# The slot numbers' broadcast moved, c split into two tiles, and the last two tiles added and stored by banks

## The chip, the cores and the metric

The kernel runs on one core of a Trainium2 chip. Its time is the device time of one execution in microseconds (us), the median of several runs. TensorE (PE) multiplies, VectorE (DVE), ScalarE (ACT) and GpSimd (POOL) do the rest, and SyncE (SP), ACT and POOL issue the DMAs.

## The reference

The input x has 8 batches of 512 rows with 2048 columns. Two layers and a residual follow, all in fp32:

```python
# layer 1: one linear map and a low-rank adapter that each batch picks by its slot number
base_out = einsum('bti,oi->bto', x, W) + b
A = lora_As[adapter_mapping]; Bm = lora_Bs[adapter_mapping]      # rank 16, 32 slots
y = base_out + einsum('btr,bro->bto', einsum('bti,bir->btr', x, A), Bm) * 2.0
# layer 2: 8 experts of rank 16; each row takes the one with the largest logit
logits = einsum('bsd,ed->bse', y, route_w)
topk_v, topk_idx = top_k(logits, 1)
route_weight = one_hot(topk_idx[..., 0], 8) * topk_v
h = einsum('bsd,erd->bser', y, A_ffn)
out = x + einsum('bser,eor->bso', route_weight[..., None] * h, Bw)
```

The kernel never builds y. What layer 2 wants of y are 136 numbers a row (128 of h and 8 logits), and these are linear in x. So W is folded into the 136 projections once (c, 2048 x 136), and each row tile is multiplied with c. The output is x plus a product of 128 numbers a row with Bw.

## The kernel before, in words

**Start.** POOL issues the broadcast of the eight slot numbers to all partitions (it_i, line 92), then fills an identity and three index tables. SP loads W in 16 chunks of 128 rows (1 MB each, load_w, line 103) and, between them, the projections (pj). ACT and DVE each reorder one half of every chunk (chunk_w, line 286), and PE folds it (fold_w, line 297) into the six PSUM tiles pc of the pool ps_c, one bank each. Beside this, from chunk 4 on, the slot numbers become row indices (line 165), by which POOL gathers the adapters. At chunk 11 DVE places the adapters A of batches 0 and 1 in c (line 379). At the last chunk the six pc tiles are copied into c (the tile cm, line 307), in turn by ACT and DVE: five with three column blocks each, the sixth with one. Then the pools of the fold close and ps_h (two banks) and ps_o (two tiles of two banks) open on the banks of ps_c; ps_s keeps its two.

**Main loop.** There are 32 row tiles, two half steps each; n counts the half steps, h is the half. For a tile t: the 16 products with c (heads, line 409), DVE's turn of the low-rank part (turn_low) and its addition on PE (add_low, line 433), DVE's choice of the expert (route, lines 446 to 454, which ends with wh), PE's transpose of wh (turn_heads, line 464, pw), ACT's copy of it (keep_heads, line 469, whT), the product with Bw in two halves of 1024 columns (delta, line 492), DVE's addition to x (add_delta, line 505) and the store (line 516). POOL and ACT shuffle quadrants of x (line 254) and DVE transposes them (line 239) for later tiles. Every two tiles SP loads x (line 122).

**Order.** The whole kernel stands under `manual_schedule`: each engine issues its instructions in the order in which the Python code emits them. What one engine waits for of another is derived from the tiles. Within one half step the order is:

```python
        if h == 0 and 0 < t <= NT:
            route(t - 1)
        tp, hp = piece(n - 1)
        if tp >= 0:
            add_delta(tp, hp)
        turn_x(t + 1, h)
        if h == 1 and 0 < t <= NT:
            keep_heads(t - 1)
```

Then come the shuffles, turn_low and delta. In the steps n = 63 and 64 a call stands between the first and the second product of delta: add_low(31), and turn_heads(31).

**End.** Tile 30 is added in halves of 1024 columns and stored by SP in halves. Tile 31 (the last) has its two halves cut into pieces in single banks: 512 and 512 columns in two banks of ps_h, then 512, 256 and 256 in ps_o, ps_o and ps_s. Each piece is added and stored by itself; the stores alternate between SP and ACT.

Of the kernel before, what the change touches and what calls it, by code (L numbers as in the profile page):

```python
# [9 lines left out]
F32 = mybir.dt.float32  # L10
# [8 lines left out]
def kernel(  # L19
# [29 lines left out]
    nc = tc.nc  # L49
    P = 128  # L50
    Q = 32
    NQ = P // Q
    B, T, D = x.shape
# [4 lines left out]
    R = ER // E  # L58
    NJ = D // P
# [3 lines left out]
    NT = B * TPB  # L63
# [4 lines left out]
    HN = D // 512 // 2  # L68
    NA = NP + R
    assert B * R == P and ER == P and DO == D and B == 2 * NQ  # L70

    const = ctx.enter_context(tc.tile_pool(name="const", bufs=1))
# [7 lines left out]
    ps_s = ctx.enter_context(tc.tile_pool(name="ps_s", bufs=2, space=bass.MemoryType.PSUM))  # L80
# [8 lines left out]


    it_i = const.tile([P, B], I32, name="it_i")
    nc.gpsimd.dma_start(out=it_i, in_=itok.to_broadcast([P, B]))
    pj = wpool.tile([P, NO, NP], F32, name="pj")
    proj_v = proj.rearrange("(c p) e -> p c e", p=P)

# [118 lines left out]
    def fill_constants():  # L214

        nc.vector.memset(one, 0.0)
        nc.vector.memset(one[:, :, R : R + 1], 1.0)

        nc.vector.tensor_reduce(
            own4, mask.rearrange("p (g h) -> p g h", h=2), AX.X, ALU.add  # L220
        )
        for k in range(2):
            h = const.tile([P, NQ, Q], F32, name=f"hls_{k}")
            nc.vector.memset(h, 0.0)
            nc.vector.tensor_copy(h[:, :, R : R + 1], own4.unsqueeze(2))
            hls.append(h)

    cm = const.tile([P, NJ, NA + R], F32, name="cm")  # L230
    ad_aT = const.tile([P, NJ, P], F32, name="ad_aT")
    ad_bT = tpool.tile([P, NJ, P], F32, tag="t", name="ad_bT")
    g4 = const.tile([P, B, NP], F32, name="g4")
# [58 lines left out]
    def fold_w(oc):  # L292
        for q, (pc, (j0, n)) in enumerate(zip(pcs, groups)):
            for k in range(n):

                h, j = divmod(j0 + k, HJ)
                nc.tensor.matmul(  # L297
                    pc[:, k, :],
                    wv_tiles[oc, h][:, j, :],
                    pj[:, oc, :],  # L300
                    start=(oc == 0 and k == 0),
                    stop=(oc == NO - 1),
                    skip_group_check=True,
                )
            if oc == NO - 1:
                copy = nc.scalar.copy if q % 2 == 0 else nc.vector.tensor_copy
                copy(cm[:, j0 : j0 + n, R:NA], pc[:, :n, :])  # L307


    bp = wpool.tile([P, NP], F32, name="bp")  # L310
# [42 lines left out]
    for oc in range(NO):  # L353
        if oc + 1 < NO:
            chunk_w(oc + 1)
        fold_w(oc)
        if oc == 2:
            fill_constants()
        if oc == 4:
            load_adapters_b()  # L360
        if oc == 7:
            load_adapters_a()
        if 8 <= oc < 12:
            turn_adapters(oc - 8)
        if oc in (9, 10):
            fold_bias(range(8 * (oc - 9), 8 * (oc - 8)))
        if oc == 8:
            load_x(0)
            shuffle(0, moves[6:], nc.gpsimd.tensor_copy)
        if oc == 11:  # L370
            nc.sync.dma_start(out=fb, in_=ffn_b)
            load_x(1)
            load_x(2)
            project_bias()
        if oc in (10, 11):
            turn(ad_aT, ad_ar, oc - 10)
        if oc == 11:
            for b in range(2):
                nc.vector.tensor_copy(cm[:, :, ds(b * NA, R)], ad_aT[:, :, ts(b, R)])
        if oc == 12:  # L380
            project_adapters()
        if oc in (12, 13, 14):
            shuffle(0, moves[2 * (oc - 12) : 2 * (oc - 11)], nc.scalar.copy)
        if oc == 14:
            for h in range(2):
                turn_x(0, h)
    wctx.close()
    ps_h = ctx.enter_context(tc.tile_pool(name="ps_h", bufs=2, space=bass.MemoryType.PSUM))
# [10 lines left out]
    po_tiles = {}  # L399
# [4 lines left out]
    def heads(t, j0, j1):  # L404
        s = batch_of(t) % 2
        if j0 == 0:
            ph_tiles[t] = ps_h.tile([P, 512], F32, tag="h", name=f"ph_{t}")[:, :NA]
        for j in range(j0, j1):
            nc.tensor.matmul(  # L409
                ph_tiles[t],  # L410
                xT_tiles[t][:, j, :],
                cm[:, j, ds(s * R, NA)],
                start=(j == 0),
                stop=(j == NJ - 1),
            )
# [15 lines left out]
    def add_low(t):  # L431
        b = batch_of(t)
        nc.tensor.matmul(  # L433
            ph_tiles[t][:, ds((1 - b % 2) * R, NP)],
            hT_tiles.pop(t),
            g4[:, b, :],
            start=False,
            stop=True,
            skip_group_check=True,
        )  # L440
# [21 lines left out]
    def turn_heads(t):  # L462
        pw = ps_s.tile([P, P], F32, tag="s", name=f"pw_{t}")
        nc.tensor.transpose(pw, wh_tiles.pop(t), ident)  # L464
        pw_tiles[t] = pw

    def keep_heads(t):
        whT_tiles[t] = small.tile([P, P], F32, tag="whT", name=f"whT_{t}")
        nc.scalar.copy(whT_tiles[t], pw_tiles.pop(t))  # L469

    def delta(t, h, within=None):

        c0 = h * D // 2
        if t < NT - 1:
            po = ps_o.tile([P, HN, 512], F32, tag="o", name=f"po_{t}_{h}")
            cuts = [(512, po[:, k, :]) for k in range(HN)]
            adds = [(ds(c0, D // 2), po.rearrange("p n d -> p (n d)"))]
        else:

            def bank(pool, tag, n):  # L480
                shape = [P, HN, 512] if tag == "o" else [P, 512]
                b = pool.tile(shape, F32, tag=tag, name=f"pe_{tag}")
                return n, (b[:, 0, :] if tag == "o" else b)[:, :n]

            if h == 0:
                cuts = [bank(ps_h, "h", 512), bank(ps_h, "h", 512)]
            else:
                cuts = [bank(ps_o, "o", 512), bank(ps_o, "o", 256), bank(ps_s, "s", 256)]
            adds = []
        c = c0  # L490
        for n, part in cuts:
            nc.tensor.matmul(part, whT_tiles[t], fb[:, ds(c, n)], start=True, stop=True)  # L492
            if t == NT - 1:
                adds.append((ds(c, n), part))
            c += n
            if within:
                within()
                within = None
        po_tiles[t, h] = adds

    def add_delta(t, h):
        u, k = divmod(t, TPU)
        for m, (cols, part) in enumerate(po_tiles.pop((t, h))):
            xs = x_tiles[u][:, k, cols]
            nc.vector.tensor_tensor(xs, xs, part, ALU.add)  # L505
            if t == NT - 1:
                store(t, cols, nc.scalar if m % 2 else nc.sync)
        if t == NT - 2:
            store(t, ts(h, D // 2))
        elif t < NT - 2 and h == 1:  # L510
            store(t, ds(0, D))

    def store(t, cols, eng=nc.sync):
        u, k = divmod(t, TPU)
        b, r = divmod(t, TPB)
        eng.dma_start(out=out[b, ts(r, P), cols], in_=x_tiles[u][:, k, cols])

    def piece(n):

        return divmod(n - 3, 2) if 0 <= n - 3 < 2 * NT else (-1, -1)  # L520
# [15 lines left out]
    for n in range(2 * NT + 4):  # L536
        t, h = divmod(n, 2)
        if t < NT:

            heads(t, h * HJ, h * HJ + HJ // 2)  # L540
            if n == 2:
                add_low(0)
            if n == 3:
                turn_heads(0)
            heads(t, h * HJ + HJ // 2, (h + 1) * HJ)
# [8 lines that stand above are left out]
        u, ms = shuffle_slot(n)  # L554
        shuffle(u, ms, nc.gpsimd.tensor_copy if n == 2 else nc.scalar.copy)
        if h == 1 and t < NT:
            turn_low(t)
        last = n in (2 * NT - 1, 2 * NT)
        if last:

            delta(*piece(n), (lambda: add_low(t)) if h else (lambda: turn_heads(t - 1)))
        elif piece(n)[0] >= 0:
            delta(*piece(n))
        if h == 1 and 0 < t < NT and not last:
            add_low(t)
        if h == 1 and t < NT:
            b, k = divmod(t, TPB)
            if k == 0 and 0 < b < B - 1:
                nc.gpsimd.tensor_copy(
                    cm[:, :, ds((b + 1) % 2 * NA, R)], ad_aT[:, :, ts(b + 1, R)]  # L570
                )
        if h == 0 and 1 < t <= NT and not last:
            turn_heads(t - 1)
        tq, hq = piece(n - 5)
        u, k = divmod(tq, TPU)
        if tq >= 0 and hq == 1 and k == TPU - 1 and u + XB < NU:
            load_x(u + XB)
# [48 lines left out]
```

## Time and profile before

| what | us |
|---|---|
| median of 3 runs | 334.65 (334.64 to 334.68) |
| the profiled execution's own time | 334.58 |
| its span | 332.8 |
| PE busy | 323.9 |
| DVE busy | 233.7 |
| ACT busy | 171.0 |
| POOL busy | 136.3 |
| PE idle between W's first and second chunk | 1.14 |
| PE idle between the fold and the first head product | 0.48 |
| from the last add's start to the end of the span | 5.8 |

A line of the timeline gives the start, the duration, the engine, the line of the code, the operation, what it writes and reads with shapes, how many instructions are merged in it, and in brackets how long the engine was idle before it and what ended that. PEld are the weight loads of PE. A name with q, such as ACTq, is the engine's sequencer, here issuing a DMA. All times in the text are from the start of the span.

### The profile page before, as it was taken

Reading aid. Unit: us, or ns where it says so; the run is one execution under the profiler, and the core shown is the slowest. Engines: PE = TensorE matmul, PEld = TensorE weight load, DVE = VectorE, ACT = ScalarE, POOL = GpSimd, SP = SyncE. Lnnn points to the kernel's source line nnn. Section 1 sums busy time; section 2 is a strip of 40 time slices with the busy share of each in tenths; the row PEclk is TensorE's granted clock in tenths of the full one; section 3 lists DMA queues with packets and bytes.
Section 4 is the critical chain, followed back from the end, with each engine's and each line's share of the span. In section 5 each row is a group of like instructions: output and inputs, shape, how many; then the busy total and the mean of one; then the engine's idle time right before and its main releaser. Section 6 shows DMA issues by size and latency. Waiting matters only on the chain.

```text
span 332.8 us, 5119 instructions
## 1 busy us (share of the span) xinstructions
PE 323.9 (97%) x1968; PEld 260.4 (78%) x1968; DVE 233.7 (70%) x425; ACT 171.0 (51%) x193; POOL 136.3 (41%) x143
## 2 busy tenths in 40 slices
PE   8899999999999999999999999999999999999992
PEld 8899999999777777777777777777777777777751
DVE  1133386476877877887878888888878777877753
ACT  3223236646857548565656575757566576630000
POOL 2001503989781609263535536262809081600000
PEclk9999999999999999999999999999999999999999
DMA  7999999958633394857676675849493949333336
GB/s 218 399 405 418 420 407 424 418 221 306 272 161 142 119 391 147 373 173 331 214 292 251 255 291 214 325 183 366 171 376 161 378 174 392 130 126 128 127 145 234
DMA packets 15800, 88.83 MB, mean 267 GB/s; under 512 B 1680, under 2 KB 4640, under 8 KB 5536
## 3 DMA queue, kind: packets, MB, share of 16 engines
q1 hardware_dynamic: 14544, 85.80, 65.7%
q0 software_dynamic: 528, 2.11, 2.0%
q10 hardware_dynamic: 704, 0.60, 0.6%
q8 instruction: 15, 0.25, 0.3%
q14 instruction: 9, 0.07, 0.1%
HBM read 54.88 MB, written 33.62 MB: 266 GB/s over the span
## 4 chain that ended last, share of the span: by engine, by line
PE 94%; DMA 3%; DVE 0%; ACT 0%; SPq 0%; issue 0%; DVEq 0%
PE ph L409 40%; PE po L492 32%; PE pc L297 17%; DMA w<-in_w_dram 3%; PE ph L433 2%; PE pg L342 1%; PE pw L464 1%; PE pbT L324 1%; PE pe_h L492 1%; ACT wv L286 0%; DVE x L505 0%; PE pe_o L492 0%; SPq L103 0%; DVEq L622 0%; DVE cm L307 0%
## 5 line engine op out<-in xcount | busy, mean ns | idle before, releaser
L254 POOL COPY xq<-x 32x1024 f32<-32x1024 f32 x121 | 126.2, 1043 | 118.2 <-DMA x<-in_x_dram 83.9
L254 ACT COPY xq<-x 32x1024 f32<-32x1024 f32 x135 | 140.9, 1043 | 17.9 <-DMA x<-in_x_dram 11.1
L409 PE MATMUL ph<-cm,xT 128*128 128x152 f32 x1024 | 142.6, 293 | 0.5 <-DVE cm L307 0.5
L409 PEld LDWEIGHTS ph<-cm,xT 128*128 128x128 f32 x1024 | 135.1, 190 | 9.3 <-issue 8.7
L492 PE MATMUL po<-fb,whT 128*128 128x512 f32 x248 | 116.7, 592 | 0.0
L505 DVE TENSOR_TENSOR x<-x,po 128x1024 f32<-128x1024 f32 x62 | 75.0, 1210 | 5.6 <-PE po L492 5.5
L239 DVE STREAM_TRANSPOSE xT<-xq 128x1024 f32<-128x1024 f32 x64 | 78.8, 1235 | 0.1
L492 PEld LDWEIGHTS po<-fb,whT 128*128 128x128 f32 x248 | 43.2, 190 | 29.2 <-issue 28.9
L297 PE MATMUL pc<-pj,wv 128*128 128x136 f32 x512 | 60.7, 279 | 1.5 <-ACT wv L286 1.1
L297 PEld LDWEIGHTS pc<-pj,wv 128*128 128x128 f32 x512 | 59.8, 190 | 1.9 <-ACT wv L286 1.3
L469 ACT COPY whT<-pw 128x128 f32<-128x128 f32 x32 | 8.5, 266 | 88.7 <-PE pw L464 88.7
L286 DVE COPY wv<-w 128x1024 f32<-128x1024 f32 (+1 forms) x17 | 13.5, 799 | 29.9 <-PE pc L297 16.1
L446 DVE TENSOR_REDUCE top<-ph 128x1 f32<-128x8 f32 x32 | 5.3, 167 | 37.5 <-PE ph L433 37.5
L286 ACT COPY wv<-w 128x1024 f32<-128x1024 f32 (+1 forms) x17 | 16.8, 996 | 27.9 <-DMA w<-in_w_dram 20.6
L433 PEld LDWEIGHTS ph<-g,hT 128*128 128x128 f32 x64 | 12.0, 190 | 15.0 <-issue 12.2
L452 DVE TENSOR_SCALAR rw<-rank,win,top 128x8 f32<-128x8 f32 x32 | 15.5, 484 | 1.2
L433 PE MATMUL ph<-g,hT 128*128 128x136 f32 x64 | 12.7, 280 | 0.0
L428 DVE STREAM_TRANSPOSE hT<-hls 128x128 f32<-128x128 f32 x32 | 10.0, 311 | 1.1
L173 POOL DMA_INDIRECT raw<-in_cond_b_dram,brow_i x1 | 1.0, 1032 | 23.6 <-DVE brow_i L172 23.6
L464 PEld LDWEIGHTS pw<-ident,wh 128*128 128x128 f32 x32 | 4.5, 140 | 7.7 <-issue 5.0
L454 DVE TENSOR_TENSOR wh<-ph,rw 128x128 f32<-128x128 f32 x32 | 9.3, 292 | 1.1
L464 PE MATMUL pw<-ident,wh 128*128 128x128 f32 x32 | 8.7, 273 | 0.0
(70 smaller groups left out, 81.1 us busy)
## 6 DMA issues: line engine op xcount, KB each, us to landing
x<-in_x_dram SPq DMA_DIRECT2D x32, 1024.0 KB, 8.9
out_dram<-x SPq DMA_DIRECT2D x30, 1024.0 KB, 4.8
w<-in_w_dram SPq DMA_DIRECT2D x16, 1024.0 KB, 11.8
fb<-in_ffn_b_dram SPq DMA_DIRECT2D x1, 1024.0 KB
out_dram<-x SPq DMA_DIRECT2D x2, 512.0 KB, 2.6
pj<-in_proj_dram SPq DMA_DIRECT2D x2, 272.0 KB, 11.4
out_dram<-x SPq DMA_DIRECT2D x2, 256.0 KB, 3.1
g<-g_dram SPq DMA_DIRECT2D x4, 68.0 KB, 2.5
```

The source lines that it names most:

```text
L239: nc.vector.transpose(dst[:, ts(h, HJ), :].rearrange("p j (g t) -> p g j t", t=Q), src.rearrange("p g (j a) -> p g j a", a=Q)[:, :, ts(h, ...
L254: copy(xq_tiles[u][ts(i, Q), :, g, :], x_tiles[u][ts(g, Q), :, ts(i, DQ)])
L286: copy(dst[:, ts(k, n)], wr[:, ds(h * HJ + k * n, n)])
L297: nc.tensor.matmul(pc[:, k, :], wv_tiles[oc, h][:, j, :], pj[:, oc, :], start=(oc == 0 and k == 0), stop=(oc == NO - 1), skip_group_check= ...
L409: nc.tensor.matmul(ph_tiles[t], xT_tiles[t][:, j, :], cm[:, j, ds(s * R, NA)], start=(j == 0), stop=(j == NJ - 1),)
L428: nc.vector.transpose(hT, h.rearrange("p g s -> p (g s)"))
L433: nc.tensor.matmul(ph_tiles[t][:, ds((1 - b % 2) * R, NP)], hT_tiles.pop(t), g4[:, b, :], start=False, stop=True, skip_group_check=True,)
L452: nc.vector.tensor_scalar(rw, rank, win, top, ALU.is_equal, ALU.mult)
L454: nc.vector.tensor_tensor(wh.rearrange("p (e r) -> p e r", r=R), ph[:, :ER].rearrange("p (e r) -> p e r", r=R), rw.unsqueeze(2).to_broadca ...
L464: nc.tensor.transpose(pw, wh_tiles.pop(t), ident)
L492: nc.tensor.matmul(part, whT_tiles[t], fb[:, ds(c, n)], start=True, stop=True)
L505: nc.vector.tensor_tensor(xs, xs, part, ALU.add)
```

## The change

It has three parts.

- The issue of the broadcast it_i moves from the head of the program to the point behind fold_w(2), after fill_constants. It stays on POOL.
- c becomes two tiles, one with the first 12 column blocks and one with the last 4. Each head product reads the tile that its block is in. Placing an adapter in c takes two copies instead of one: on DVE for batches 0 and 1, on POOL for the six others.
- The last two tiles, 30 and 31, are both added and stored by pieces in single banks, and a table says which pools these come from. The stores alternate between SP and ACT by the piece's place in its call of add_delta. The first piece of (30, 0) is added and stored right after its delta, in step 63; the second follows in step 64 after route(31), where its place in the call is 0 again.

```diff
-    nc.gpsimd.dma_start(out=it_i, in_=itok.to_broadcast([P, B]))
...
+    JC = NJ * 3 // 4
+    cms = [const.tile([P, n, NA + R], F32, name=f"cm_{n}") for n in (JC, NJ - JC)]
+
+    def cm(j):
+        return cms[j // JC][:, j % JC, :]
+
+    def place_a(b, copy):
+        for k, part in enumerate(cms):
+            n = part.shape[1]
+            copy(part[:, :, ds(b % 2 * NA, R)], ad_aT[:, ds(k * JC, n), ts(b, R)])
...
-                copy(cm[:, j0 : j0 + n, R:NA], pc[:, :n, :])
+                copy(cms[j0 // JC][:, ds(j0 % JC, n), R:NA], pc[:, :n, :])
...
         if oc == 2:
             fill_constants()
+            nc.gpsimd.dma_start(out=it_i, in_=itok.to_broadcast([P, B]))
...
-                nc.vector.tensor_copy(cm[:, :, ds(b * NA, R)], ad_aT[:, :, ts(b, R)])
+                place_a(b, nc.vector.tensor_copy)
...
-                cm[:, j, ds(s * R, NA)],
+                cm(j)[:, ds(s * R, NA)],
...
+    def bank(tag, n):
+
+        pool, shape = {
+            "h": (ps_h, [P, 512]), "s": (ps_s, [P, 512]), "o": (ps_o, [P, HN, 512])
+        }[tag]
+        b = pool.tile(shape, F32, tag=tag, name=f"pe_{tag}")
+        return n, (b[:, 0, :] if tag == "o" else b)[:, :n]
+
+
+    ends = {
+        (NT - 2, 0): (("o", 512), ("o", 512)),
+        (NT - 2, 1): (("h", 512), ("s", 512)),
+        (NT - 1, 0): (("h", 512), ("o", 512)),
+        (NT - 1, 1): (("o", 512), ("h", 256), ("s", 256)),
+    }
+
     def delta(t, h, within=None):
 
         c0 = h * D // 2
-        if t < NT - 1:
+        if (t, h) in ends:
+            cuts = ends[t, h]
+        else:
             po = ps_o.tile([P, HN, 512], F32, tag="o", name=f"po_{t}_{h}")
             cuts = [(512, po[:, k, :]) for k in range(HN)]
...
+            po_tiles[t, h] = [(ds(c0, D // 2), po.rearrange("p n d -> p (n d)"))]
         c = c0
-        for n, part in cuts:
+        for cut in cuts:
+            if (t, h) in ends:
+                cut = bank(*cut)
+                po_tiles.setdefault((t, h), []).append((ds(c, cut[0]), cut[1]))
+            n, part = cut
             nc.tensor.matmul(part, whT_tiles[t], fb[:, ds(c, n)], start=True, stop=True)
...
+    def add_delta(t, h, n=None):
+
         u, k = divmod(t, TPU)
-        for m, (cols, part) in enumerate(po_tiles.pop((t, h))):
+        pieces = po_tiles[t, h]
+        po_tiles[t, h] = pieces[n:] if n else []
+        for m, (cols, part) in enumerate(pieces[:n]):
             xs = x_tiles[u][:, k, cols]
             nc.vector.tensor_tensor(xs, xs, part, ALU.add)
-            if t == NT - 1:
+            if (t, h) in ends:
                 store(t, cols, nc.scalar if m % 2 else nc.sync)
-        if t == NT - 2:
-            store(t, ts(h, D // 2))
-        elif t < NT - 2 and h == 1:
-            store(t, ds(0, D))
+            elif h == 1:
+                store(t, ds(0, D))
...
             delta(*piece(n), (lambda: add_low(t)) if h else (lambda: turn_heads(t - 1)))
+            if h == 1:
+                add_delta(*piece(n), 1)
...
-                nc.gpsimd.tensor_copy(
-                    cm[:, :, ds((b + 1) % 2 * NA, R)], ad_aT[:, :, ts(b + 1, R)]
-                )
+                place_a(b + 1, nc.gpsimd.tensor_copy)
```

More of the change, by code (lines that the diff above doesn't have):

```diff
@@ L226, in fill_constants @@
             hls.append(h)
-    cm = const.tile([P, NJ, NA + R], F32, name="cm")
+    JC = NJ * 3 // 4
[6 more added lines that the diff above has]
+            copy(part[:, :, ds(b % 2 * NA, R)], ad_aT[:, ds(k * JC, n), ts(b, R)])
     ad_aT = const.tile([P, NJ, P], F32, name="ad_aT")
@@ L469, in keep_heads @@
         nc.scalar.copy(whT_tiles[t], pw_tiles.pop(t))
+    def bank(tag, n):
[10 more added lines that the diff above has]
+    }
     def delta(t, h, within=None):
         c0 = h * D // 2
-        if t < NT - 1:
+        if (t, h) in ends:
+            cuts = ends[t, h]
+        else:
             po = ps_o.tile([P, HN, 512], F32, tag="o", name=f"po_{t}_{h}")
             cuts = [(512, po[:, k, :]) for k in range(HN)]
[L477 to L489, printed above, removed]
-        c = c0
-        for n, part in cuts:
+            po_tiles[t, h] = [(ds(c0, D // 2), po.rearrange("p n d -> p (n d)"))]
+        c = c0
+        for cut in cuts:
[3 more added lines that the diff above has]
+            n, part = cut
             nc.tensor.matmul(part, whT_tiles[t], fb[:, ds(c, n)], start=True, stop=True)
-            if t == NT - 1:
-                adds.append((ds(c, n), part))
             c += n
@@ L498, in delta @@
                 within = None
-        po_tiles[t, h] = adds
-    def add_delta(t, h):
+    def add_delta(t, h, n=None):
         u, k = divmod(t, TPU)
-        for m, (cols, part) in enumerate(po_tiles.pop((t, h))):
+        pieces = po_tiles[t, h]
+        po_tiles[t, h] = pieces[n:] if n else []
+        for m, (cols, part) in enumerate(pieces[:n]):
             xs = x_tiles[u][:, k, cols]
             nc.vector.tensor_tensor(xs, xs, part, ALU.add)
-            if t == NT - 1:
+            if (t, h) in ends:
                 store(t, cols, nc.scalar if m % 2 else nc.sync)
-        if t == NT - 2:
-            store(t, ts(h, D // 2))
-        elif t < NT - 2 and h == 1:
-            store(t, ds(0, D))
+            elif h == 1:
+                store(t, ds(0, D))
     def store(t, cols, eng=nc.sync):
```

## The prediction

> **What bounds the kernel now.** The page first: its busy times, then the chain that ended last.
>
> ```profile
> PE 323.9 (97%) x1968; PEld 260.4 (78%) x1968; DVE 233.7 (70%) x425; ACT 171.0 (51%) x193; POOL 136.3 (41%) x143
> ...
> PE 94%; DMA 3%; DVE 0%; ACT 0%; SPq 0%; issue 0%; DVEq 0%
> ```
>
> TensorE is the chain from 11.42 us to 326.05 us, so only three places are open: before 11.42, a gap at 73, and what follows 326.05. The change has one edit in each. I then read the timeline of each place. The start:
>
> ```profile
> 1.28 0.72 POOL L92 DMA_DIRECT2D it_i<-in_itok_dram  x1 [0.83 <-POOLq L611]
> ...
> 10.32 1.05 ACT L286 COPY wv<-w 128x1024 f32<-128x1024 f32 x1 [3.35 <-DMA w<-in_w_dram]
> ...
> 11.42 14.75 PE L297 MATMUL pc<-pj,wv 128*128 128x136 f32 x125 [1.14 <-ACT wv L286]
> ...
> 21.42 1.05 ACT L286 COPY wv<-w 128x1024 f32<-128x1024 f32 x1 [3.63 <-DMA w<-in_w_dram]
> ```
>
> PE stands 1.14 us for W's second chunk, which comes at 10.32. The table of stretches (PE, PEld, DVE, ACT, POOL, clock, DMA share, GB/s) and the queues of the same 1.5 us say why:
>
> ```profile
> 4.00:5.50 1.50, 1.50 (x14) 1.50 (x14) 0.00 (x0) 0.00 (x0) 0.00 (x0) 1.00 1.02 419
> 5.50:7.00 1.50, 1.17 (x11) 0.98 (x10) 0.76 (x2) 1.14 (x2) 0.00 (x0) 1.00 1.07 54
> ```
>
> ```profile
> q0 software_dynamic: 16, 0.00, 90.7%
> ```
>
> The DMA engines are fully busy but move 54 GB/s instead of 419: the broadcast's 16 packets (one an engine, 256 bytes) hold them for 0.907 x 1.5 = 1.36 us. They begin at 5.57, which is 3.57 us after POOL finished the issue at 2.00.
>
> The gap at 73:
>
> ```profile
> 72.79 0.50 ACT L307 COPY cm<-pc 128x408 f32<-128x408 f32 x1 [0.89 <-PE pc L297]
> 73.02 0.30 DVE L307 COPY cm<-pc 128x136 f32<-128x136 f32 x1 [0.34 <-PE pc L297]
> ...
> 73.47 5.41 PE L409 MATMUL ph<-cm,xT 128*128 128x152 f32 x40 [0.48 <-DVE cm L307]
> ```
>
> The end:
>
> ```profile
> 320.81 0.17 DVE L446 TENSOR_REDUCE top<-ph 128x1 f32<-128x8 f32 x1 [0.59 <-PE ph L433]
> ...
> 322.14 0.14 PEld L464 LDWEIGHTS pw<-ident,wh 128*128 128x128 f32 x1 [0.48 <-DVE wh L454]
> ...
> 322.69 0.27 ACT L469 COPY whT<-pw 128x128 f32<-128x128 f32 x1 [4.79 <-PE pw L464]
> ...
> 323.30 1.88 PE L492 MATMUL pe_h<-fb,whT 128*128 128x512 f32 x4
> 323.50 1.22 DVE L505 TENSOR_TENSOR x<-x,po 128x1024 f32<-128x1024 f32 x1 [0.28 <-PE po L492]
> ...
> 325.95 1.53 ACTq L516 DMA_DIRECT2D out_dram<-x  x2
> ```
>
> whT of tile 31 is ready at 322.96, 0.34 us before PE can use it. After 324 the stores fill the DMA engines without a break (352, 381 and 310 GB/s in the three 2-us stretches from 324). The last is issued at 327.45, its packets run from 329.33 to 330.38, it lands at 330.99, the span ends at 332.77. An unhindered store has its first packet 0.83 us after its issue (323.25 to 324.08), so the last one queued about 1.0 us.
>
> **What the Trainium skill says.** "PSUM — Partial Sum Buffer", Engine vs sequencer instructions: the queues of ScalarE, VectorE and GpSimd are strictly first in, first out. "DMA: Bandwidth & Descriptors", Anatomy of one DMA: a DMA's semaphore wait takes place on the sequencer that issues it. Together: an instruction behind a store that waits, waits too. The trace agrees for SP (218.8 us of store waits, with x loads behind them); on ACT it shows only stores behind a waiting store. Same page, Issuing engines are not separate DMA queues: all queues share the same engines. The trace agrees: ACT's store of tile 31, issued at 325.95, starts its packets at 327.56, as the SP store before it ends. "PSUM — Partial Sum Buffer", Specifications: 8 banks. ps_s has 2 and ps_c 6, so ps_h can only take banks of ps_c.
>
> **The change, part by part.** The sum is made on the profiled execution: span 332.8, own time 334.58; the median of the runs is 334.65.
>
> *The broadcast.* It is written beside chunk three, but nothing on POOL holds it there: ahead of it stand only the identity and three iotas, which ended at 2.89 behind the 0.71-us issue and so end at 2.18 without it. Issue 2.18 to 2.90, packets 3.57 us later (3.2 for the next indirect load, 27.57 to 30.78): 6.1 to 6.5. W's second chunk, whose packets ended at 9.85, would end at 9.85 - 1.36 = 8.49 without the broadcast; it still catches it and pays the same 1.36 us. Even behind that chunk, little is won: the fifth lands at 21.32, its copy ends at 22.46, and PE wants it at 11.42 + 3 x 3.71 = 22.55. With the DMA engines saturated, every broadcast ahead of 21.3 leaves that landing where it is, so the gain is at most 0.09. Bounds 0 to -1.1 (the whole stall); I take 0. it_f needs the numbers at 25.3, far later than the 10 or so at which they land.
>
> *c in two tiles.* The first ph product would need the copies up to the fourth (DVE, 72.09 + 0.58 = 72.67), before PE's last pc at 72.98: at most 73.47 - 72.98 = 0.48 is won. But ps_h is opened on ps_c's banks, and as I read the allocator, a pool on a closed pool's bytes waits for all users of that pool; the fifth and sixth copies, of ACT and DVE, are users. The view of before agrees with either reading, as both waits end with those copies. Bounds 0 to -0.48; I take 0. The added copies (two on DVE near 57, one more on POOL in each of six batches, 0.40 us for the whole one) lie beside PE work; POOL is 41% busy, and DVE's next chunk copy, 58.25 to 59.81, is wanted by PE at 61.86. Were that cover gone they would cost about 0.3 us each.
>
> *The end.* Three things happen.
> (1) The first add of tile 30 (512 columns, 0.68 us) now stands ahead of route(31). It starts at 320.51, when its bank is done; route starts 0.60 later, at 321.11 instead of 320.81: +0.30. wh is late by that, and PE's transpose, which took wh as it came, by 0.14 to 0.30. The second bank of (30, 1) ends at 323.60 to 323.76 instead of 323.46.
> (2) Stores alternate by piece. The second piece of (30, 1) goes to ACT, and in the loop add_delta(30, 1) stands ahead of keep_heads(31). ACT's queue is therefore: this store, whT, two stores. The store waits for the add: 323.76 + 0.04 + 0.68 = 324.48, issue 324.51 to 324.87 (0.36 as at 325.95). Behind it the whT copy starts at 324.96 instead of 322.69 and ends at 325.22; weights 0.05 later, so PE starts tile 31's products at about 325.3 to 325.45 instead of 323.30. PE stands, and everything after is late by 2.0 to 2.15 us. Behind whT wait all four products of tile 31, their adds and stores.
> (3) Tile 30's stores start early (321.2, 323.0, 323.6, 324.5 instead of 323.25 and 324.75), so with the stall the DMA engines are free when the last three stores come: issued at 328.96, 329.29 and 329.62. First packet at 328.96 + 0.83 = 329.79. The three took 8 x (106 + 56 + 53) ns = 1.7 us of packets an engine, and 2.13 from first packet to last end; 1.54 to 2.13 gives 331.3 to 331.9, against 330.38. That is +0.95 to +1.55; with the low end of (1), +0.8. I take +1.1.
>
> Sum: 0 + 0 + 1.1, so span 333.9, profiled time 335.7, and on the median 335.75.
>
> **The rivals.** *Faster: the waiting store doesn't hold whT.* Place: ACT between 323 and 325. Then only (1) remains, PE is 0.3 late, and the three stores start not at 328.25 but as soon as ACT's store ends, about 327.95: end 329.75, -0.6, 334.0. For it: the trace has no ACT copy behind a waiting store. Against: the queue rule above and SP's behaviour. It decides at a PE delay s where 327.62 + s + 1.8 = 330.38, s about 0.95: whT ready later than about 324.2 loses.
> *The split of c wins its 0.48:* 335.75 - 0.48 = 335.3. For it: the wait is named after the cm copy. Against: the banks.
> *The broadcast leaves the W chunks alone:* 335.75 - 1.1 = 334.65. For it: 1.36 us of engines held; against: POOL's early issue and the fifth chunk's 0.09.
> *The change doesn't do what it says* is part of my forecast, for the broadcast's place and c's wait.
>
> **How the numbers follow.** 0.2% is 0.67 us, about what a measurement here can tell from no change: faster is below 333.98, slower above 335.32. Forecast 0.73, own range 335.35 to 336.3, all slower. Split wins 0.11, 334.9 to 335.5, of it 0.03 slower. ACT not held 0.09, 333.7 to 334.2, of it 0.07 faster. Broadcast hidden 0.05: 0.03 same, 0.02 faster together with the split. Worse than 336.3: 0.02. Faster 0.09, same 0.13, slower 0.78. The range 334.9 to 336.3 leaves out ACT not held, most of broadcast hidden, and the worse case.
>
> **What would show it.** The broadcast's packets at 6.1 to 6.5 with the same loss of GB/s, W's second chunk still at 10.3; ph still waiting 0.48 at 73; in the end, a PE stall of 1.5 to 2 us before pe products with ACT's whT after a store near 324.5, and last packets at 331.3 to 331.9. A whT near 323.0, or PE on ph at 73.0, or on the second chunk at 10.3 and never short again, would make it wrong.

## The result, and the profile after

| | before | after |
|---|---|---|
| median of 22 runs each, us | 334.63 (334.47 to 334.79) | 335.19 (334.96 to 335.76) |
| ratio | | 1.0019, 95% interval 1.0012 to 1.0025 |
| profiled execution, own time and span | 334.58, 332.8 | 335.51, 333.7 |

The kernel is 0.56 us slower. The profiled execution lies 0.3 us above the median, and that part is visible at its start: PE goes on to W's second chunk 0.31 later (11.73 against 11.42, below) and the first head product follows as late (73.78 against 73.47). I take this 0.31 off when the two traces are compared further on; it is an estimate, as one execution stands for each kernel.

The page after, busy times and the chain:

```profile
PE 324.5 (97%) x1968; PEld 260.4 (78%) x1968; DVE 234.9 (70%) x429; ACT 171.0 (51%) x193; POOL 136.8 (41%) x149
...
PE 94%; DMA 3%; DVE 1%; ACT 0%; issue 0%; SPq 0%; ACTq 0%; DVEq 0%
```

PE is the chain as before. New in it are a per cent of DVE and a piece of ACTq, ACT's sequencer at a store. The start, from the timeline:

```profile
1.58 0.75 POOL L369 DMA_DIRECT2D it_i<-in_itok_dram  x1
...
10.64 1.04 ACT L296 COPY wv<-w 128x1024 f32<-128x1024 f32 x1 [3.46 <-DMA w<-in_w_dram]
...
11.73 15.44 PE L307 MATMUL pc<-pj,wv 128*128 128x136 f32 x131 [1.23 <-ACT wv L296]
...
21.40 1.05 ACT L296 COPY wv<-w 128x1024 f32<-128x1024 f32 x1 [3.27 <-DMA w<-in_w_dram]
```

The broadcast is issued 0.30 us later than before (1.58 against 1.28), not beside the third chunk. W's second chunk comes no earlier, and PE stands for it as before, here 1.23 us. The stretches (PE, PEld, DVE, ACT, POOL, clock, DMA share, GB/s) show the same hole in the transfers, moved by a microsecond:

```profile
5.50:7.00 1.50, 1.16 (x11) 0.97 (x10) 0.76 (x2) 0.96 (x2) 0.00 (x0) 1.00 1.49 292
7.00:8.50 1.50, 1.50 (x16) 1.50 (x15) 0.00 (x0) 0.18 (x1) 0.00 (x0) 1.00 0.54 177
```

In the packet records the broadcast's 16 packets of 256 bytes begin between 5.8 and 7.0, not 6.1 to 6.5; eleven of them begin between 6.6 and 7.0, and ten of these last 1.4 to 1.7 us, inside W's second chunk (5.25 to 9.90). The gap at 73 is unchanged in spite of the two tiles, 0.48 us:

```profile
73.10 0.50 ACT L317 COPY cm<-pc 128x408 f32<-128x408 f32 x1 [0.89 <-PE pc L307]
73.33 0.30 DVE L317 COPY cm<-pc 128x136 f32<-128x136 f32 x1 [0.35 <-PE pc L307]
...
73.78 1.40 PE L420 MATMUL ph<-cm,xT 128*128 128x152 f32 x9 [0.48 <-DVE cm L317]
```

The end, from the timeline:

```profile
320.82 0.69 DVE L526 TENSOR_TENSOR x<-x,pe_o 128x512 f32<-128x512 f32 x1 [0.29 <-PE pe_o L513]
...
321.43 0.16 DVE L457 TENSOR_REDUCE top<-ph 128x1 f32<-128x8 f32 x1
...
323.98 0.69 DVE L526 TENSOR_TENSOR x<-x,pe_s 128x512 f32<-128x512 f32 x1
324.70 0.36 ACTq L535 DMA_DIRECT2D out_dram<-x  x1
325.15 0.27 ACT L480 COPY whT<-pw 128x128 f32<-128x128 f32 x1 [6.94 <-DVE x L526]
325.47 0.30 PEld L513 LDWEIGHTS pe_h<-fb,whT 128*128 128x128 f32 x2 [2.36 <-ACT whT L480]
325.47 1.12 PE L513 MATMUL pe_h<-fb,whT 128*128 128x512 f32 x2 [1.53 <-ACT whT L480]
```

Read it from below: PE stood 1.53 us for whT; ACT had been idle for 6.94 us before that copy, and what ended its wait was an addition on DVE (323.98), through the store in between (324.70). The chain of waits names the same links with nothing between them:

```profile
323.98 0.70 DVE x L526
...
324.70 0.36 ACTq L535
...
325.15 0.28 ACT whT L480
...
325.47 1.12 PE pe_h L513 x2
```

The last packets end at 331.86 (330.38 before) and the last store lands at 332.52 (330.99). So the last landing is 1.53 us later, but the span only 0.97. From the last landing to the end of the span it took 1.78 us before and 1.22 after: 0.56 us that no step of the prediction had.

### The profile page after: what moved, and what is told of

Same layout as the page of the kernel before. It is cut to its first block, busy times and chain, and to the rows that moved or that the text cites. A ratio compares the mean times of both kernels' runs of the same rounds, so it can differ in the third digit from the quotient of the medians.

```text
span 333.7 us, 5133 instructions
## 1 busy us (share of the span) xinstructions
PE 324.5 (97%) x1968; PEld 260.4 (78%) x1968; DVE 234.9 (70%) x429; ACT 171.0 (51%) x193; POOL 136.8 (41%) x149
## 4 chain that ended last, share of the span: by engine, by line
PE 94%; DMA 3%; DVE 1%; ACT 0%; issue 0%; SPq 0%; ACTq 0%; DVEq 0%
PE ph L420 40%; PE po L513 31%; PE pc L307 17%; DMA w<-in_w_dram 3%; PE ph L444 2%; PE pg L352 1%; PE pw L475 1%; PE pe_o L513 1%; PE pe_h L513 1%; PE pbT L334 1%; DVE x L526 1%; ACT wv L296 0%; PE pe_s L513 0%; SPq L102 0%; ACTq L535 0%
## 5 line engine op out<-in xcount | busy, mean ns | idle before, releaser
L513 PE MATMUL po<-fb,whT 128*128 128x512 f32 x240 | 112.8, 592 | 0.0
L526 DVE TENSOR_TENSOR x<-x,po 128x1024 f32<-128x1024 f32 x60 | 72.5, 1209 | 5.3 <-PE po L513 4.9
L513 PEld LDWEIGHTS po<-fb,whT 128*128 128x128 f32 x240 | 41.9, 190 | 28.7 <-issue 28.7
```

## The experiments

Each time is the median of its runs, and the ratio stands against runs of the kernel before on the same chip (334.61 to 334.69).

**The three parts alone.** Does each do what the prediction gave it? The first is the broadcast's move:

```diff
-    nc.gpsimd.dma_start(out=it_i, in_=itok.to_broadcast([P, B]))
...
             fill_constants()
+            nc.gpsimd.dma_start(out=it_i, in_=itok.to_broadcast([P, B]))
```

> The kernel before with the broadcast's move alone. My theory: POOL issues it right behind the iotas, it still lies among the packets of W's second chunk, and that chunk lands as late as before or up to 0.3 us later; time 0 to +0.3 against before. Rival (the move takes it out of the way of the W chunks): PE starts on the second chunk at about 10.3 instead of 11.4 and the time falls by about 1.1. Its effect on the end of the span: none, POOL executes as many instructions as before.

334.62, ratio 0.9999 (0.9991 to 1.0007): nothing, as forecast. From the last landing to the end of the span: 1.79.

The second is c in two tiles (cms, cm(j) and place_a as in the change).

> The kernel before with c in two tiles alone. My theory: the first head product still stands 0.48 us, since ps_h takes banks of ps_c and waits for all copies; that part is 0. The stretch from the last store's landing to the end of the span was 1.78 us before and 1.22 after the change; part of it, 0.44, is POOL's, whose drain began late in the kernel before. If that goes by POOL's instruction count (143 before, 149 with the split), this run is 0.4 faster than before with the wait at 73 us unchanged. Rival one (the split wins the wait): PE's wait at 73 is gone, -0.45, and the end unchanged. Rival two: neither, 0.

334.25, ratio 0.9986 (0.9980 to 0.9993). It is faster, but not where the edit is; the timeline at 73 us:

```profile
73.01 0.30 DVE L317 COPY cm<-pc 128x136 f32<-128x136 f32 x1 [0.34 <-PE pc L307]
...
73.45 0.76 PE L419 MATMUL ph<-cm,xT 128*128 128x152 f32 x4 [0.48 <-DVE cm L317]
```

The wait is there in full, 0.48, and the stretch behind the last landing is 1.35. Rival one falls.

The third is the end by banks, on two queues (bank, ends, delta, add_delta and the call in step 63 as in the change).

> The kernel before with the third part alone (tiles 30 and 31 by banks, on two queues). My theory: ACT's store stands ahead of whT of tile 31, PE stands about 1.6 us, the last store lands 1.1 to 1.2 later, and with POOL's instructions as before the end of the span keeps its 1.78 us: +1.1 against before, slower than the whole change. Rival (the end of the span got shorter because of the stores themselves): +0.6.

335.73, ratio 1.0032 (1.0020 to 1.0044), which is +1.04, and 1.66 us behind the last landing. The parts add up: -0.07 - 0.44 + 1.04 = +0.53, against +0.56 for the whole.

**whT ahead of the additions.** In the third part alone, the copy of whT of tile 31 is emitted before the additions of (30, 1):

```diff
+        if n == 2 * NT + 1:
+            keep_heads(t - 1)
         tp, hp = piece(n - 1)
         if tp >= 0:
             add_delta(tp, hp)
         turn_x(t + 1, h)
-        if h == 1 and 0 < t <= NT:
+        if h == 1 and 0 < t < NT:
             keep_heads(t - 1)
```

> The third part alone, with the copy of whT of tile 31 written ahead of the additions of (30, 1), so ahead of ACT's store of that piece; nothing else differs from the third part alone. My theory: whT at about 323.0 to 323.3, PE at most 0.3 late, the last stores find the DMA engines freer than before: -0.5 to -0.7 against before. Rival (the stall is due to the earlier first addition, which makes route and the transpose late, or to PE's banks): PE still stands over 1 us and the time is +0.6 or more.

333.78, ratio 0.9974 (0.9963 to 0.9984): -0.91, and 1.95 below the same part without it. The timeline:

```profile
322.99 0.27 ACT L469 COPY whT<-pw 128x128 f32<-128x128 f32 x1 [4.96 <-PE pw L464]
...
323.60 1.02 PE L502 MATMUL pe_h<-fb,whT 128*128 128x512 f32 x2
...
324.52 0.36 ACTq L524 DMA_DIRECT2D out_dram<-x  x1
```

ACT's store is issued when it was, at about 324.5; with whT ahead of it PE doesn't stand. The banks, the early first addition and the second queue are all still in, so none of these by itself is what costs; it is the order on ACT's queue. The gain was somewhat above the 0.5 to 0.7 that I gave; the last packets end at 329.94 (330.38 before).

**The waiting store alone.** In the kernel before, the store of the second half of tile 30 goes to ACT, and nothing else changes:

```diff
         if t == NT - 2:
-            store(t, ts(h, D // 2))
+            store(t, ts(h, D // 2), nc.scalar if h else nc.sync)
```

> The kernel before with one word changed: the store of tile 30's second half is issued by ACT instead of SP. It stands ahead of whT of tile 31 on ACT and waits for the addition that ends at 324.7. My theory (a store that waits holds what is behind it on its engine): whT starts at about 325.2 instead of 322.7, PE stands about 2 us, and since the last stores then find the DMA engines freer, the time rises by 1.2 to 1.6. Rival (a waiting store doesn't hold ACT's copies): 0.

336.12, ratio 1.0046 (1.0030 to 1.0061): +1.48. The timeline:

```profile
323.45 1.22 DVE L505 TENSOR_TENSOR x<-x,po 128x1024 f32<-128x1024 f32 x1 [0.28 <-PE po L492]
324.70 0.37 ACTq L516 DMA_DIRECT2D out_dram<-x  x1
325.17 0.27 ACT L469 COPY whT<-pw 128x128 f32<-128x128 f32 x1 [7.32 <-DVE x L505]
...
325.49 1.98 PE L492 MATMUL pe_h<-fb,whT 128*128 128x512 f32 x4 [2.08 <-ACT whT L469]
```

One word moves whT from 322.7 to 325.2 and gives PE a stall of 2.08 us. That settles the faster rival of the prediction: a store that waits on ACT does hold ACT's copies. Of the 2.08 us, 1.48 reach the end: the last store is issued 2.29 later than before (329.74 against 327.45), but the last packets end only 1.45 later (331.83 against 330.38), as it no longer queues so long for the DMA engines.

**The wait at 73.** Two kernels let ps_h and ps_o wait only for the users of their own banks, the first with c in one tile as before, the second with c in two:

```diff
-    ps_h = ctx.enter_context(tc.tile_pool(name="ps_h", bufs=2, space=bass.MemoryType.PSUM))
+    ps_h = ctx.enter_context(tc.tile_pool(name="ps_h", bufs=2, space=bass.MemoryType.PSUM, reuse_waits="tile"))
```

(The same word on ps_o.)

> The kernel before with c in one tile, but with the two PSUM pools that follow the fold (ps_h and ps_o) each waiting only for the users of its own banks instead of all users of the closed pool. My theory: c's own tile still ties the first head product to the last copy, so PE's wait at 73 us stays 0.48 and the time is that of before. Rival (reads of c are tied to the copies of the columns they read): the wait goes, -0.45.

333.92, ratio 0.9979 (0.9972 to 0.9986). My expectation failed. The timeline with c in one tile:

```profile
72.79 0.50 ACT L307 COPY cm<-pc 128x408 f32<-128x408 f32 x1 [0.89 <-PE pc L297]
72.82 1.46 PE L409 MATMUL ph<-cm,xT 128*128 128x152 f32 x10
73.02 0.30 DVE L307 COPY cm<-pc 128x136 f32<-128x136 f32 x1 [0.34 <-PE pc L297]
```

PE starts ph at 72.82, ahead of the last two copies, with no wait. The reads of c were never tied to the whole tile; the wait was the pool's alone. The 0.72 us won are more than the wait of 0.48, but the interval reaches from 0.47 to 0.94.

> The split of c together with the pools that wait only for the users of their own banks. My theory (in the split alone the wait was the pool's): PE's wait at 73 us goes, so -0.45 against the split alone and, with POOL's shorter end, -0.85 to -0.9 against before. Rival (the wait has another cause, PE's own start): as the split alone, -0.4 against before.

333.86, ratio 0.9972 (0.9960 to 0.9983): the wait is gone here too. It is 0.39 below the split alone, but no more than 0.06 below c in one tile, and -0.78 against before is a little less than I gave. Its trace has the short end of the split (1.35 us, see POOL's end), so it should be 0.43 below c in one tile as well. The runs neither show that nor rule it out: the interval reaches from 0.57 to 1.34 us faster than before, and the seven times from 333.21 to 334.21.

**POOL's end.** The split of c, which left its wait standing, was 0.44 faster. It adds six instructions on POOL. So the kernel before, with six tiny copies of POOL that nobody reads, one beside each placing of an adapter (pad is a new tile of 8 columns):

```diff
+                nc.gpsimd.tensor_copy(pad, own)
```

> The kernel before with one tiny copy on POOL (8 columns, read by nobody) added in each of the six batches, so that POOL runs as many instructions as with the split of c. My theory (the split alone was faster through POOL's end, not through the wait at 73 us): -0.4, with PE's wait at 73 unchanged and POOL's drain following at once. Rival (it is the split of c itself, or its place in memory): 0.

334.16, ratio 0.9989 (0.9982 to 0.9995), -0.45, with PE's wait at 73 still 0.48. What the trace holds of the end, with POOL's records counted with the sequencer's own:

```text
                       POOL    last      end of   between   POOL's last drains:    last fetch of
                       records landing   span               begin, duration (us)   instructions at
before                 201     330.99    332.77   1.78      332.06, 0.225          332.7
broadcast moved        201     330.91    332.70   1.79      331.99, 0.226          332.7
third part alone       201     332.29    333.95   1.66      333.25, 0.225          333.9
third part, whT ahead  201     330.51    332.18   1.67      331.47, 0.226          332.2
split of c alone       207     331.03    332.38   1.35      331.80, 0.097          307.9
six tiny copies        207     330.83    332.18   1.35      331.60, 0.097          307.8
after (whole change)   207     332.52    333.74   1.22      333.16, 0.097          308.2
slot numbers by PE     200     330.25    331.85   1.59      330.96, 0.097          332.1
```

A drain is the instruction that the records call DRAIN, among the last of each engine. The last row is the first kernel under "The broadcast" below.

With 201 records POOL begins its final drain about 0.26 us after SP's and takes 0.225 us for it, and a packet of 8 KB of instructions is fetched as the span ends; with 207 the drain stands beside SP's (0.05 ahead), takes 0.097, and there is a fetch at 284 instead. These 0.31 and 0.13 us make up the 0.43 between 1.78 and 1.35. It therefore goes by POOL's instructions, and not by what the split does to c.

The row with 200 records says more. There the drain is on time and short, but POOL pauses for the same 0.31 us one instruction later, ahead of the clearing of the semaphores (331.39; the drain ended at 331.05). One instruction fewer moves the pause on by one place, six more leave none at the end, so it seems to belong to a place in POOL's stream of instructions. What POOL waits for there stays open. It isn't the arrival of the fetch at the end, for that packet begins at 332.75, after the late drain has ended (332.29).

The third part shortens the stretch by another 0.1: SP waits for eight semaphores in turn, 0.06 us each, and there the store that lands last is the third in that turn and no longer the first.

**The broadcast.** The prediction blamed 1.36 us of held DMA engines on its packets. Here ACT loads the eight numbers into partition 0 alone, and PE multiplies them by the warm-up's matrix of ones behind the fold of chunk 3:

```diff
-    nc.gpsimd.dma_start(out=it_i, in_=itok.to_broadcast([P, B]))
+    nc.vector.memset(it_i, 0)
...
+    nc.scalar.dma_start(out=it_i[:1], in_=itok)
...
+        if oc == 3:
+            nc.vector.tensor_copy(it_z, it_i)
+            it_p = ps_s.tile([P, B], F32, tag="s", name="it_p")
+            nc.tensor.matmul(it_p, warm, it_z, start=True, stop=True)
```

> The kernel before without the broadcast by DMA: ACT issues one packet of 32 bytes into partition 0 of a zeroed tile, and PE multiplies it by the matrix of ones of the warm-up after the fold of chunk 3, so that every partition has the numbers. My theory (the broadcast's packets hold all DMA engines for 1.36 us): W's second chunk lands at about 8.9 to 9.1 instead of 10.3, PE goes on to it at 10.3, and the time falls by 0.9 to 1.2. Rival (the DMA engines lose that time to something else, or the fifth chunk binds anyway): 0 to -0.2.

333.74, ratio 0.9973 (0.9962 to 0.9984), -0.90. The timeline, and the stretch in which the engines had moved 54 GB/s:

```profile
6.78 14.99 PE L299 MATMUL pc<-pj,wv 128*128 128x136 f32 x128
...
8.77 1.05 ACT L288 COPY wv<-w 128x1024 f32<-128x1024 f32 x1 [1.58 <-DMA w<-in_w_dram]
```

```profile
5.50:7.00 1.50, 1.50 (x11) 1.50 (x11) 0.77 (x2) 0.95 (x2) 0.00 (x0) 1.00 1.03 426
```

W's second chunk is there at 8.77 instead of 10.32, and PE folds from chunk to chunk without a stop. Of the 0.90, about 0.2 is the shorter end in the table above (1.59 against 1.78), so the start is worth about 0.7. That is less than the stall of 1.14, as the fold itself begins later in this trace (6.78 against 6.31); why stays open.

Is it the small pieces on POOL's queue, or that all read one address? The next kernel adds, at the broadcast's old place, a load of 128 rows of 32 bytes that lie apart:

```diff
+    pad = const.tile([P, B], F32, name="pad")
+    nc.gpsimd.dma_start(out=pad, in_=bias[:, :B])
```

> The run with the slot numbers through PE, with one more DMA at the old place of the broadcast: POOL loads 128 rows of 32 bytes that lie apart (columns of the bias) into a tile that nobody reads. Same queue, same place, same number and size of pieces as the broadcast; only the addresses differ. My theory (the 1.36 us come from 128 reads of the same 32 bytes): W's second chunk stays early and the time that of the run with the slot numbers through PE, -0.9 against before. Rival (small pieces on POOL's queue, or its first use, hold the engines): the stall is back, 0.

333.94, ratio 0.9978 (0.9971 to 0.9984): -0.67, less than the 0.9 that I gave, but here the end takes 1.73, nearly as long as before, so about 0.6 is the start's. W's second chunk, the stretch, and the broadcast's queue between 4 and 9 us:

```profile
8.83 1.05 ACT L290 COPY wv<-w 128x1024 f32<-128x1024 f32 x1 [1.73 <-DMA w<-in_w_dram]
```

```profile
5.50:7.00 1.50, 1.50 (x9) 1.50 (x9) 0.76 (x2) 1.04 (x2) 0.00 (x0) 1.00 0.99 405
```

```profile
q0 software_dynamic: 32, 0.00, 0.5%
```

Of these 32 packets 16 have 256 bytes, as in the broadcast, and 16 have 4. Those of 256 bytes now take 18 ns each in the packet records (1,361 ns on average as a broadcast of one address), and the hole is gone. Queue, size and place are the same; what differs is the source. It is the shared address, and not a slow place of the slot numbers: ACT's single read of them takes 9 ns.

**The first addition's place.** In the third part with whT ahead, the first piece of tile 30 is added behind route(31) again, and both pieces of (30, 0) go to SP:

```diff
-            if h == 1:
-                add_delta(*piece(n), 1)
...
-                store(t, cols, nc.scalar if m % 2 else nc.sync)
+                store(t, cols, nc.scalar if m % 2 and (t, h) != (NT - 2, 0) else nc.sync)
```

> The third part with whT ahead, but tile 30's first piece added in step 64 behind route(31) with the second (both stored by SP). My theory: route(31) starts 0.3 us earlier, PE's transpose 0.14 to 0.3 earlier, so -0.15 to -0.3 against the third part with whT ahead. Rival (the DMA engines set the end, and the first store now starts later): 0 or up to +0.2.

333.70, ratio 0.9974 (0.9964 to 0.9984), the same ratio as with the early addition. The 0.15 to 0.3 that I gave don't show, though the intervals are too wide to exclude them. The two traces say more. At the store before, they are 0.19 us apart (318.66 here, 318.85 with the early addition). With that taken off, route(31) starts 0.31 earlier here (320.75 against 321.25), but the last packets end only 0.03 earlier (329.72 against 329.94). So in these traces the early addition makes route late and costs next to nothing at the end.

**The mended change.** The whole change with whT ahead, the pools by banks and the slot numbers through PE:

> The whole change with three mends: the slot numbers through PE instead of the broadcast, ps_h and ps_o waiting only for the users of their own banks, and whT of tile 31 ahead of the additions of (30, 1). My theory: the gains add up, -0.9 (start), -0.48 (the wait at 73), -0.4 (POOL's end), -0.6 to -0.9 (the last stores): 332.0 to 332.3. Rival (the early start is lost again to W's later chunks or to x): above 332.8.

332.00, ratio 0.9917 (0.9904 to 0.9931): 2.6 us faster than before and 3.2 faster than the change. That is within the forecast of 332.0 to 332.3; five runs with an interval of 2.3 to 3.2 us against before can't say that every gain is there in full.

## Why the prediction was right, and where it was off

The forecast was 335.75 in 334.9 to 336.3, slower; measured, 335.19, slower by 0.17% (0.12 to 0.25). That it gets slower, and by which mechanism, was right. The likeliest case was 0.56 too high, and one term of the sum explains most of it.

That the range held is luck in part. 335.19 lies below the range of the forecast itself, 335.35 to 336.3. It is inside the wider one only because that reaches down to 334.9 for the rival that the split wins its 0.48. That rival fell; POOL's end, which the prediction didn't have, happens to be worth about as much. By the prediction's own bound of 0.2% (335.32) the median counts as the same, to which it gave 0.13. The interval, 0.12 to 0.25%, lies across that bound.

*The broadcast, taken at 0.* Right: 0.9999 alone. It was issued even earlier than I said (1.58 instead of 2.18), as POOL's fills begin at 0.74 where the broadcast was issued at 1.28 before, and still fell into W's second chunk. That its packets hold all engines was right too. But the bound of 0.09 for every place ahead of the fifth chunk was not tried.

*c in two tiles, taken at 0.* The wait at 73 stayed 0.48, as forecast, and its cause was named rightly: the pool's rule. I was wrong to hold that without this rule the split would win 0.48; c in one tile wins it as well. And the part was not 0 in time: -0.44 came from POOL's shorter end. This is the term that I mis-sized. I priced the added copies on POOL only as work beside PE, and never asked what they do to the end of the span, where the late drain could be seen in the trace of before.

*The end, step (1).* route starts 0.31 later (321.43 - 0.31 against 320.81), as forecast. Its price at the end, for which the prediction gave up to 0.3, was about 0.03 in the two traces compared above.

*Step (2).* The link was right: the store at 324.39 with the 0.31 taken off (forecast 324.51), whT at 324.84 (324.96), PE's products 1.86 later than before (2.0 to 2.15, a little too much). The waiting store alone, put into the kernel before, reproduces it.

*Step (3).* The last packets end 331.86 - 0.31 = 331.55 (forecast 331.3 to 331.9), 1.17 later than before (I took 1.1). The third part alone gave +1.04.

So the sum should have read 0 - 0.44 + 1.1 = +0.66, against 0.56 measured. The chance of 0.78 for slower by over 0.2% came from the sum without POOL's term.

The rivals: the one that ACT isn't held falls (+1.48 with the store alone), that of the split falls (0.48 still there), that of the hidden broadcast falls (0.9999).

## What to carry to other kernels

A second DMA queue on an engine that computes isn't free: a store put there waits for its data at the head of that engine's queue, so look at what is emitted behind it and who waits for that. Before a tile is split to shorten a wait, find out which rule makes the wait; here it was the pool that took over the banks, and one word there won what the split could not. Where a DMA spreads one small row over all partitions, look at what the DMA engines move meanwhile, not only at the bytes it has.

## What the hardware showed unexpectedly

- 128 pieces of 32 bytes read from one address held all 16 DMA engines for about 1.4 us (16 packets of 1,361 ns on average); the same pieces from addresses apart took 18 ns a packet.
- Six tiny instructions more on POOL, far from the end, made the kernel 0.45 us faster (0.17 to 0.60 by the interval): POOL's final drain began 0.31 us earlier against SP's and was 0.13 us shorter, and a fetch of instructions moved from the very end of the span to 284 us. With one instruction fewer the pause of 0.31 us stood one instruction later.
